# Attention values summed over two row halves, in two PSUM banks, in layers 1 to 3 of a four-layer gated cross-attention kernel

## The chip, the cores and the metric

One Trainium2 chip; the kernel runs on one of its cores. The metric is the device time of one execution in microseconds (us). A core has TensorE (PE; its weight loads are shown apart as PEld), VectorE (DVE), ScalarE (ACT), GpSimd (POOL) and SyncE (SP, which only issues DMAs here). They run side by side, each through its own instructions in order, and wait for each other by semaphores. TensorE writes its results to PSUM, which the kernel uses as eight banks of 128 rows x 512 f32 numbers; the other operands lie in SBUF.

## What is computed

Four layers, each a cross-attention and a feed-forward part, on `x` of 16 batches x 56 tokens x 256, with a context of 16 x 1500 x 64:

```python
x = x + tanh(g_xattn[l]) * xattn_l(layernorm(x), ctx)
x = x + tanh(g_ffn[l])   * ffn_l(layernorm(x))
```

In layers 1 to 3 the attention is multi-head latent attention with 16 heads. With the context `kv_rope` (rotated, 1500 x 64 for a batch), it comes down to

```python
scores = einsum('bhsr,bhlr->bhsl', q_r, k_r)       # l: 1500 keys
attn   = softmax(scores)
ctx_c  = einsum('bhsl,bld->bhsd', attn, kv_rope)   # the "values": 64 numbers a query
out    = (ctx_c through w_kc_kv) @ Wo.T
```

The kernel folds the weights so that a query is 64 numbers that meet `kv_rope` itself, for keys and for values. The feed-forward parts are a mixture of experts (layers 0, 2, 3) and an fp8-rounded matrix (layer 1). All of the attention is in f32.

## The kernel before

**Tiles and steps.** `attention_mla(l, ...)` (L698) is called for l = 1, 2, 3. The 16 batches are 8 tiles of two batches. A tile has 896 queries for each of the two batches (16 heads x 56 tokens), cut into 7 blocks of 128 (`QT`), so a layer has 56 steps `Step(t, j)`, the three layers 168. The 1500 keys are 12 chunks (`KC`) of 125 (`KP`). `kv[125, tile, chunk, batch, 64]` holds the context by keys; `kvT[128, 1500]` holds it turned, batch b in rows 64b to 64b+63.

**A step** has these parts, for both batches b = 0, 1:

- `scores` (L760): for each third z of the keys (500 of them) one matmul a batch, with 64 rows: batch 0 into bank `sp0[z]`, batch 1 into a bank of `sp1`. The two batches use different halves of TensorE's rows.
- `maxima0` (L772, L774), `maxima1` (L777) on VectorE, `exps0` (L783, three instructions) and `exps1` (L792) on ScalarE: exponentials `p` and their sums `den`.
- `invert` (L803 to L811): the sums are added on GpSimd, inverted and turned on VectorE (L805, L807), and go through DRAM by DMAs of SP's queue (L809, L811) to be repeated over 64 rows each in `rep`.
- `turned(n)`, n = 0 to 5 (L822): four 125x128 blocks of `p` are turned by TensorE into one bank, and `keep_turned(n)` copies the bank to `pT`: n = 0, 1 by VectorE (L830), the rest by ScalarE (L832).
- `values` (L840): for each chunk and batch one matmul of 125 rows, `kv` (125 x 64) as weights and `pT` (125 x 128) streaming; batch b writes rows 64b to 64b+63 of one bank, so the two batches use different halves of the columns. All 12 chunks are summed there.
- `keep` (L851): VectorE multiplies the sum by `rep` into `ctxT`, one piece a batch, two in the block j = 3 that has columns of both halves of the heads.

**Order.** It is written out by hand: `in_order` keeps the order of the program on each engine. Pass k of the loop issues the scores, maxima and first exponentials of step k, then the values of step k-2, then six times a turn of step k-1 with its copy, with `exps1` and `invert` of step k before the third. Between them, generators (`go("X")`, "Z", "R", "E") issue the parts that follow a finished tile: `project` (L863, 8 matmuls on `ctxT`), the next layer's normalisation, the router, the fp8 matrix.

**Keys of layer 1.** There `kvT` of the next tile is made on TensorE: `keys(t, z)` (L745) turns four chunks into a bank and ScalarE copies them (L748), in the passes with j = 2, 3, 4, after the scores and ahead of the first exponentials. The result is also stored (L750) and read back in layers 2 and 3.

**Banks.** Eight: `sp0` three, `sp1` three, and two that `misc()` gives in turn. Turns n = 1, 2, 3 use `sp0[0..2]`, whose exponentials are done; n = 0, 4, 5 and the values use `misc()`. The values' bank is also lent: `room(n)` gives its columns from 128 on to the generators.

## Time and profile before

| | |
|---|---|
| three runs | 2300.48, 2300.88, 2303.32 us; median 2300.88 |
| the profiled execution | 2298.12 us, its span 2296.3 us |
| TensorE's granted clock, mean over the span | 0.977; 1.00 in the stretches of the three attention layers |
| attention layers 1, 2, 3 (from the span's start) | about 335 to 820, 943 to 1365, 1619 to 2118 us |
| scores on TensorE, L760 | x2016, mean 596 ns, busy 471.7 us |
| turns on TensorE, L822 | x4032, mean 281 and 274 ns, busy 292.6 and 265.3 us |
| values on TensorE, L840 | x8064, mean 275 ns, busy 478.2 us |
| products on VectorE, L851 | x384, mean 272 ns, busy 104.3 us |
| copies of turned probabilities, ScalarE, L832 | x672, mean 595 and 619 ns |
| GpSimd in all | busy 346.3 us, 15% |

Every f32 matmul that computes shows as two instructions; a turn shows as one. The busy time of TensorE counts overlapping matmuls once, and an instruction's duration runs from its start to its modelled end, so durations of neighbours overlap: what a phase costs is read from start to start in the timeline. A timeline line merges equal instructions in a row; its columns are the start, the time to the end of the last, the engine and line, and how many. In the table of groups the last columns are the idle time of the engine just ahead of them and what ended it.

### The profile page before, as it was taken

To read this page: it belongs to the slowest core of one execution; us is meant where nothing else is said; L and a number is where in the kernel's file an instruction comes from. 1 tells how busy PE (TensorE), PEld (TensorE's weight loads), DVE (VectorE), ACT (ScalarE), POOL (GpSimd) and SP (SyncE) were. 2 spreads that over 40 slices of the span, in tenths; PEclk is the share of its full clock that TensorE was granted. 3 is DMA by queue.
4 is the path that set the end of the run, shared out by engine and by line. 5 is a ranking of instruction groups with operands and counts; after the bars stand their busy time and mean duration, and the time that the engine had idled before them with its cause. 6 is when DMAs were issued, how large, how long until landed. Compare 5 with 4: busy or idle time off the path is not lost. (4 is left out here: it accounts for less than half of the span.)

```text
span 2296.3 us, 47100 instructions
## 1 busy us (share of the span) xinstructions
PE 2198.5 (96%) x17838; PEld 1598.8 (70%) x17846; DVE 1562.3 (68%) x3627; ACT 1221.7 (53%) x2675; POOL 346.3 (15%) x678
## 2 busy tenths in 40 slices
PE   8879999999999999999999999989999999999698
PEld 5647657777777784457777777745677777777465
DVE  5658457777777878767777777624677777777332
ACT  4313357666666653366666666514666666666132
POOL 1225600000000004410000000000001111101234
PEclk9779999999999999999999999999999999999799
DMA  9545450000000002100000000154001100000465
GB/s 273 183 136 163 141 158 23 22 22 23 16 15 22 23 23 81 57 20 22 25 24 24 25 12 23 49 206 142 20 22 31 30 30 21 27 22 18 135 196 168
DMA packets 106681, 153.48 MB, mean 67 GB/s; under 512 B 18319, under 2 KB 76696, under 8 KB 105417
## 3 DMA queue, kind: packets, MB, share of 16 engines
q1 hardware_dynamic: 97299, 131.83, 18.9%
q0 software_dynamic: 7600, 17.14, 2.3%
q8 instruction: 146, 2.39, 0.4%
q10 hardware_dynamic: 1542, 1.34, 0.2%
q14 instruction: 94, 0.77, 0.1%
HBM read 111.73 MB, written 40.48 MB: 66 GB/s over the span
## 5 line engine op out<-in xcount | busy, mean ns | idle before, releaser
L783 ACT ACTIVATE p<-s_ps,nm 128x500 f32<-128x500 f32 x504 | 335.2, 674 | 402.1 <-DVE nm L774 396.3
L840 PEld LDWEIGHTS m_ps<-pT,kv 125*64 125x64 f32 x8064 | 437.0, 137 | 112.5 <-issue 108.8
L840 PE MATMUL m_ps<-pT,kv 125*64 125x128 f32 x8064 | 478.2, 275 | 3.7 <-ACT pT L832 2.5
L772 DVE TENSOR_REDUCE part<-s_ps 128x1 f32<-128x500 f32 x504 | 341.8, 678 | 203.0 <-PE s_ps L760 200.0
L760 PE MATMUL s_ps<-kvT,qT 64*128 64x500 f32 x2016 | 471.7, 596 | 3.1 <-ACT qT L330 2.6
L760 PEld LDWEIGHTS s_ps<-kvT,qT 64*128 64x128 f32 x2016 | 182.4, 186 | 179.1 <-issue 115.6
L822 PE MATMUL m_ps<-ident,p 128*125 128x128 f32 x2016 | 292.6, 281 | 2.4 <-issue 2.4
L777 DVE TENSOR_REDUCE nm<-s_ps 128x1 f32<-128x1500 f32 x168 | 287.5, 1711 | 0.0
L822 PEld LDWEIGHTS m_ps<-ident,p 128*125 128x125 f32 x2016 | 246.2, 187 | 33.6 <-issue 28.2
L822 PE MATMUL s_ps<-ident,p 128*125 128x128 f32 x2016 | 265.3, 274 | 1.5 <-ACT p L783 1.0
L792 ACT ACTIVATE p<-s_ps,nm 128x1500 f32<-128x1500 f32 x168 | 254.5, 1515 | 4.5 <-DVE nm L777 4.4
L822 PEld LDWEIGHTS s_ps<-ident,p 128*125 128x125 f32 x2016 | 241.9, 188 | 4.0 <-ACT p L783 1.6
L832 ACT COPY pT<-s_ps 125x512 f32<-125x512 f32 x336 | 180.8, 595 | 99.7 <-PE s_ps L822 87.1
L803 POOL TENSOR_TENSOR den<-den 128x1 f32<-128x1 f32 x168 | 32.5, 193 | 1325.9 <-ACT p L783 1325.7
L832 ACT COPY pT<-m_ps 125x512 f32<-125x512 f32 x336 | 185.1, 619 | 0.0
L851 DVE TENSOR_TENSOR ctxT<-m_ps,rep 64x128 f32<-64x128 f32 (+1 forms) x384 | 104.3, 272 | 65.6 <-PE m_ps L840 52.0
L1336 PE MATMUL gu_ps<-wgu,xT 128*128 128x448 f32 (+2 forms) x344 | 138.3, 528 | 4.4 <-ACT xT L1326 4.4
L830 DVE COPY pT<-m_ps 125x512 f32<-125x512 f32 x168 | 116.2, 692 | 10.5 <-PE s_ps L822 0.5
L330 ACT COPY qT<-q_ps 64x224 f32<-64x224 f32 x124 | 69.7, 562 | 98.5 <-PE q_ps L378 67.1
L1361 POOL DMA_INDIRECT results<-y,to x78 | 92.8, 1189 | 169.3 <-ACT y L1360 116.9
L830 DVE COPY pT<-s_ps 125x512 f32<-125x512 f32 x168 | 114.4, 681 | 0.0
L1341 DVE TENSOR_TENSOR act<-gu_ps,act 128x224 f32<-128x224 f32 (+2 forms) x78 | 31.3, 401 | 120.7 <-ACT act L1340 88.8
(305 smaller groups left out, 2518.4 us busy)
## 6 DMA issues: line engine op xcount, KB each, us to landing
rows<-zero SPq DMA_DIRECT2D x16, 899.5 KB
kvT<-turned_kv SPq DMA_DIRECT2D x16, 750.0 KB
rep<-through SPq DMA_DIRECT2D x336, 32.0 KB
xrow<-rows SPq DMA_DIRECT2D x78, 128.5 KB
wgu<-in_L_wgu SPq DMA_DIRECT2D x21, 448.0 KB
wgu<-in_L_wgu SPq DMA_DIRECT2D x8, 1024.0 KB
back<-results SPq DMA_DIRECT2D x16, 448.0 KB
wq<-in_L_wq SPq DMA_DIRECT2D x24, 256.0 KB
```

The costliest lines, as they stand in the source:

```text
L760: in_order(nc.tensor.matmul(o[:, 0 : 4 * KP], qT[64 * b : 64 * b + 64, t, j * QT : (j + 1) * QT], kvTs[t][64 * b : 64 * b + 64, z * 4 * KP ...
L772: in_order(nc.vector.tensor_reduce(self.part[:, z : z + 1], sp0[z][:, 0 : 4 * KP], AX.X, ALU.max))
L777: in_order(nc.vector.tensor_reduce(self.nm[1], sp1[:, :, 0 : 4 * KP], AX.XY, ALU.max, negate=True))
L783: in_order(nc.scalar.activation(self.p[0][:, 4 * z * KP : 4 * (z + 1) * KP], sp0[z][:, 0 : 4 * KP], AF.Exp, bias=self.nm[0], accum_out=sel ...
L792: in_order(nc.scalar.activation(self.p[1].rearrange("p (z c) -> p z c", z=3), sp1[:, :, 0 : 4 * KP], AF.Exp, bias=self.nm[1], accum_out=se ...
L822: in_order(nc.tensor.transpose(ps[:, c, :], self.p[b][:, k : k + KP], ident))
L830: in_order(nc.vector.tensor_copy(o, ps))
L832: in_order(nc.scalar.copy(o, ps))
L840: in_order(nc.tensor.matmul(self.pv[64 * b : 64 * b + 64, :], kv[:, self.t, c, b, :], self.pT[:, c, b, :], start=c == 0, stop=c == KC - 1))
L851: in_order(nc.vector.tensor_tensor(ctxs[self.t][64 * a : 64 * a + 64, b, lo - 448 * a : hi - 448 * a], self.pv[64 * b : 64 * b + 64, cols] ...
L1336: in_order(nc.tensor.matmul(ps[:, s, 0:n], xT[:, k, :], wgu[:, k, s * n : (s + 1) * n], start=k == 0, stop=k == 1))
L1361: i = nc.gpsimd.indirect_dma_start(flat, bass.IndirectOffsetOnAxis(ap=to[:, 0:1], axis=0), y, None, bounds_check=B * S * top - 1, oob_is_e ...
```

## The change

Five things change together:

1. **Values.** Each chunk of 125 keys is cut into rows 0 to 63 and 64 to 124. Each matmul becomes two, with 64 and 61 rows, the lower half of the keys into one `misc()` bank (`lent`), the upper into a second (`beside`). The columns stay 64 a batch.
2. **Keep.** VectorE multiplies each of the two 128x128 sums by `rep` into SBUF (`v0`, `v1`), and GpSimd adds them into `ctxT`, in the pieces of before.
3. **Score banks rotate.** The bank of third z in step i is `sp0[(i + z) % 3]`.
4. **Turns.** As the values hold both `misc()` banks, n = 0, 1, 2 and 5 use `sp0[(k + n % 5) % 3]`, and n = 3, 4 use `misc()`.
5. **Keys of layer 1.** Four parts of three chunks, in place of three of four, in the passes with j = 2 to 5, issued after the second turn into the columns from 128 on of `beside`. In layers 2 and 3 the read of the turned keys stays at j = 2.

```diff
@@ -96,7 +96,7 @@
     def misc():
         return psm.tile([128, 512], F32, tag="m", name="m_ps")
 
-    lent = [None]
+    lent, beside = [None], [None]
 
     def room(n):
 
@@ -732,31 +732,31 @@
             ctxs = {}
             nq = 8 * TP // QT
 
-            def keys(t, z):
-
-                if l > 1:
-                    if z == 0:
-                        keys_again(t)
-                    return
+            def keys(t, z, ps=None):
+
                 if z == 0:
                     kvTs[t] = kp.tile([128, L], F32, name="kvT")
-                ps = misc()
-                for c in range(4):
+                ps = (misc() if ps is None else ps[:, QT:])[:, 0 : 3 * KP]
+                for c in range(3):
                     in_order(nc.tensor.transpose(
-                        ps[:, c * KP : (c + 1) * KP], kv[:, t, 4 * z + c].rearrange("p b e -> p (b e)"), ident[0:KP, 0:KP]
+                        ps[:, c * KP : (c + 1) * KP], kv[:, t, 3 * z + c].rearrange("p b e -> p (b e)"), ident[0:KP, 0:KP]
                     ))
-                in_order(nc.scalar.copy(kvTs[t][:, z * 4 * KP : (z + 1) * 4 * KP], ps[:, 0 : 4 * KP]))
-                if z == 2:
+                in_order(nc.scalar.copy(kvTs[t][:, z * 3 * KP : (z + 1) * 3 * KP], ps))
+                if z == 3:
                     in_order(nc.sync.dma_start(turned_kv[t], kvTs[t]))
 
             class Step:
                 def __init__(self, t, j):
                     self.t, self.j = t, j
 
+                def bank(self, z):
+
+                    return sp0[(nq * self.t + self.j + z) % 3]
+
                 def scores(self, z):
 
                     t, j = self.t, self.j
-                    for b, o in enumerate((sp0[z], sp1[:, z, :])):
+                    for b, o in enumerate((self.bank(z), sp1[:, z, :])):
                         in_order(nc.tensor.matmul(
                             o[:, 0 : 4 * KP],
                             qT[64 * b : 64 * b + 64, t, j * QT : (j + 1) * QT],
@@ -769,7 +769,7 @@
                     if z == 0:
                         self.part = ap.tile([QT, 3], F32, name="part")
                         self.nm = [ap.tile([QT, 1], F32, name=f"nm{b}") for b in range(2)]
-                    in_order(nc.vector.tensor_reduce(self.part[:, z : z + 1], sp0[z][:, 0 : 4 * KP], AX.X, ALU.max))
+                    in_order(nc.vector.tensor_reduce(self.part[:, z : z + 1], self.bank(z)[:, 0 : 4 * KP], AX.X, ALU.max))
                     if z == 2:
                         in_order(nc.vector.tensor_reduce(self.nm[0], self.part, AX.X, ALU.max, negate=True))
 
@@ -782,7 +782,7 @@
                     for z in range(3):
                         in_order(nc.scalar.activation(
                             self.p[0][:, 4 * z * KP : 4 * (z + 1) * KP],
-                            sp0[z][:, 0 : 4 * KP],
+                            self.bank(z)[:, 0 : 4 * KP],
                             AF.Exp,
                             bias=self.nm[0],
                             accum_out=self.den[:, z : z + 1],
@@ -810,16 +810,17 @@
                     for b in range(2):
                         in_order(nc.sync.dma_start(self.rep[64 * b : 64 * b + 64, :], through[b : b + 1, :].to_broadcast([64, QT])))
 
-                def turned(self, n):
+                def turned(self, n, at):
+
 
                     if n == 0:
                         self.pT = ap.tile([KP, KC, 2, QT], F32, name="pT", bufs=1)
                     z, b = n // 2, n % 2
-                    ps = sp0[n - 1] if 1 <= n <= 3 else misc()
+                    ps = misc() if n in (3, 4) else sp0[(at + n % 5) % 3]
                     ps = ps[0:KP, :].rearrange("p (c q) -> p c q", c=4)
                     for c in range(4):
-                        k = (4 * z + c) * KP
-                        in_order(nc.tensor.transpose(ps[:, c, :], self.p[b][:, k : k + KP], ident))
+                        cut = slice((4 * z + c) * KP, (4 * z + c + 1) * KP)
+                        in_order(nc.tensor.transpose(ps[:, c, :], self.p[b][:, cut], ident))
                     self.turning = ps
 
                 def keep_turned(self, n):
@@ -833,26 +834,37 @@
 
                 def values(self):
 
+
+
+                    beside[0] = misc()
                     lent[0] = misc()
-                    self.pv = lent[0][:, 0:QT]
+                    self.pv = [ps[:, 0:QT] for ps in (lent[0], beside[0])]
                     for c in range(KC):
                         for b in range(2):
-                            in_order(nc.tensor.matmul(
-                                self.pv[64 * b : 64 * b + 64, :], kv[:, self.t, c, b, :], self.pT[:, c, b, :], start=c == 0, stop=c == KC - 1
-                            ))
+                            for h, keys_of in enumerate((slice(0, 64), slice(64, KP))):
+                                in_order(nc.tensor.matmul(
+                                    self.pv[h][64 * b : 64 * b + 64, :],
+                                    kv[keys_of, self.t, c, b, :],
+                                    self.pT[keys_of, c, b, :],
+                                    start=c == 0,
+                                    stop=c == KC - 1,
+                                ))
 
                 def keep(self):
 
+                    v = [ap.tile([128, QT], F32, name=f"v{h}") for h in range(2)]
+                    for h in range(2):
+                        in_order(nc.vector.tensor_tensor(v[h], self.pv[h], self.rep, ALU.mult))
                     for a in range(2):
                         lo, hi = max(self.j * QT, 448 * a), min((self.j + 1) * QT, 448 * (a + 1))
                         for b in range(2):
                             if lo < hi:
                                 cols = slice(lo - self.j * QT, hi - self.j * QT)
-                                in_order(nc.vector.tensor_tensor(
+                                in_order(nc.gpsimd.tensor_tensor(
                                     ctxs[self.t][64 * a : 64 * a + 64, b, lo - 448 * a : hi - 448 * a],
-                                    self.pv[64 * b : 64 * b + 64, cols],
-                                    self.rep[64 * b : 64 * b + 64, cols],
-                                    ALU.mult,
+                                    v[0][64 * b : 64 * b + 64, cols],
+                                    v[1][64 * b : 64 * b + 64, cols],
+                                    ALU.add,
                                 ))
 
             def project(t):
@@ -875,7 +887,7 @@
             def at(i):
                 return steps[i] if 0 <= i < n else None
 
-            for z in range(3 if l == 1 else 0):
+            for z in range(4 if l == 1 else 0):
                 keys(0, z)
             after, wanted, pending = iter(()), "X", None
 
@@ -900,8 +912,8 @@
                     for z in range(3):
                         new.scores(z)
                         new.maxima0(z)
-                    if new.t + 1 < NT and new.j in (2, 3, 4):
-                        keys(new.t + 1, new.j - 2)
+                    if l > 1 and new.t + 1 < NT and new.j == 2:
+                        keys_again(new.t + 1)
                 if k == 0:
                     late = late()
                     next(late, None)
@@ -917,13 +929,15 @@
                         new.exps1()
                         new.invert()
                     if turn:
-                        turn.turned(i)
+                        turn.turned(i, k)
                     if i == 1:
                         if pending:
                             for _ in after:
                                 pass
                             after, wanted, pending = pending, "Z", None
                         go("Z")
+                        if l == 1 and new and new.t + 1 < NT and new.j in (2, 3, 4, 5):
+                            keys(new.t + 1, new.j - 2, beside[0])
                     if turn:
                         turn.keep_turned(i)
                     if i == 1:
```

## Prediction

> **What bounds the kernel now.** I read the busy table first, then the groups of instructions, then one step of layer 1 in the timeline, then the waits of TensorE.
>
> ```profile
> PE 2198.5 (96%) x17838; PEld 1598.8 (70%) x17846; DVE 1562.3 (68%) x3627; ACT 1221.7 (53%) x2675; POOL 346.3 (15%) x678
> ...
> L840 PE MATMUL m_ps<-pT,kv 125*64 125x128 f32 x8064 | 478.2, 275 | 3.7 <-ACT pT L832 2.5
> ...
> L760 PE MATMUL s_ps<-kvT,qT 64*128 64x500 f32 x2016 | 471.7, 596 | 3.1 <-ACT qT L330 2.6
> ```
>
> TensorE is busy 96% of the span, and its two large groups sat idle for under 4 us in all. The three attention layers (335 to 820, 943 to 1365 and 1619 to 2118 us) are 1406 us, of which the table by stretches gives TensorE 1394. The timeline of TensorE shows the order; the first step here also turns keys (L745), the second does not.
>
> ```profile
> 433.07 2.79 PE L760 MATMUL s_ps<-kvT,qT 64*128 64x500 f32 x12
> 435.79 0.65 PE L745 MATMUL m_ps<-ident,kv 125*128 125x125 f32 x4
> 436.36 2.84 PE L840 MATMUL m_ps<-pT,kv 125*64 125x128 f32 x48
> 439.13 0.70 PE L822 MATMUL m_ps<-ident,p 128*125 128x128 f32 x4
> 439.67 1.47 PE L822 MATMUL s_ps<-ident,p 128*125 128x128 f32 x12
> 440.98 1.04 PE L822 MATMUL m_ps<-ident,p 128*125 128x128 f32 x8
> 441.95 2.79 PE L760 MATMUL s_ps<-kvT,qT 64*128 64x500 f32 x12
> 444.67 2.84 PE L840 MATMUL m_ps<-pT,kv 125*64 125x128 f32 x48
> 447.44 0.70 PE L822 MATMUL m_ps<-ident,p 128*125 128x128 f32 x4
> ```
>
> From start to start, scores take 2.72 us, values 2.77, the 24 turns of probabilities 2.82: 8.30 us a step, 168 steps, no wait between them. So only TensorE's own work, or a wait that reaches it, moves the time.
>
> **The values (168 steps).** An f32 matmul is two instructions, so 24 matmuls are x48. In the single records they start in pairs, 7 ns apart (the two halves of the columns), with 109 ns from pair to pair: 24 x 109 = 2.62 us, and the rest of the 2.77 is the start of the phase. 109 ns is the streaming of 128 columns: a score instruction with 500 columns and 64 rows takes 417 ns, the same 0.83 ns a column. So fewer rows don't stream faster, and two tiles of 125 x 64 already fill the array. The change makes 96 instructions of 64 (or 61) x 64 with the same 128 columns. If four run at once, as pairs do now on two column halves (L840) and on two row halves (L760), that is 24 fours x 109 = 2.62 us again: **no gain in streaming**, and two more starts of 7 ns each: 14 ns x 168 = +2.4 us. No row shows four at once. Bounds: two at a time gives 48 x 109 = 5.23 us, +2.62 x 168 = +440; below nothing I see no reason, as the array has no idle part now. I take +2.4, by the two rows that show halves running side by side.
>
> [...] The contraction here is 125 and is cut in two, so the number of matmuls doubles with it; I follow the rows above.
>
> **The change of shape.** Between two phases of one array shape the next matmul starts 2 to 3 ns after the last one's streaming ends (turns to L863, L1640); with a change of shape it is 92 to 98 ns, plus the first weight load. That holds whether rows and columns change (L760 to L840), columns alone (L376 to L378) or rows alone (L822 to L760). Scores are 64 x 128, the values become 64 x 64, the turns 128 x 128: still three changes a step, 0. If the first cost nothing, 0.145 us x 168 = 24 us would go (second rival).
>
> **The keys of layer 1 (7 tiles).** Today three of seven steps of a tile turn four chunks each ahead of the values. Such steps take 8.88 instead of 8.30: 0.58, of which 4 x 109 ns is work and 0.14 a change of shape. Afterwards four steps turn three chunks each among the turns of probabilities: 0.33 each and no change of shape. But ScalarE's queue changes too. Today its key copy goes first:
>
> ```profile
> 436.47 0.58 ACT L748 COPY kvT<-m_ps 128x500 f32<-128x500 f32 x1 [2.49 <-PE m_ps L745]
> 436.94 0.69 ACT L783 ACTIVATE p<-s_ps,nm 128x500 f32<-128x500 f32 x1
> ...
> 439.46 1.51 ACT L792 ACTIVATE p<-s_ps,nm 128x1500 f32<-128x1500 f32 x1 [0.43 <-DVE nm L777]
> ...
> 440.96 1.06 ACT L832 COPY pT<-s_ps 125x512 f32<-125x512 f32 x2
> 441.90 1.09 ACT L832 COPY pT<-m_ps 125x512 f32<-125x512 f32 x2
> ```
>
> Afterwards it stands between the exponentials L783 and L792 and waits for the keys' turns, which come after the values and eight turns. Behind it in ScalarE's queue stand L792 and the four copies L832; for them wait the next scores' second half (L792), their second chunk (first copy) and third chunk (now the last copy), and the reciprocal. For this step, without L745 ahead: values at 435.79, turns at 438.56, keys done at 439.86 (+0.16 to be seen), the copy 440.05 to 440.41, L792 to 441.91, the copies 0.48 apart, the last ending at 443.95. TensorE has its turns done and starts the next scores at 441.71; their third chunk would start at 443.48 and waits until 443.95: **about 0.5 us**. Bounds: 0 (the copy earlier by that much) to 0.9 (0.30 for L792 adds up). Per tile: 4 x (0.33 + 0.5) - 3 x 0.58 = +1.6; x 7 = **+11 us** (-3 to +22).
>
> **Banks that rotate.** In the other steps the third chunk's bank also comes free with the last copy: that ends at 442.99 above, the third chunk starts near 443.7, so 0.7 us of cover. The first turn now waits for the first exponential (done 446.4; turn at 447.44). Both hidden; each us beyond the cover would cost 168 us.
>
> **Products and sums.** VectorE: 384 products of 64x128 (272 ns) become 336 of 128x128, the same columns, so about -13 us of busy time off the path. GpSimd gains 384 additions: its rows give 193 ns for 128x1 (L803), 319 for 112x64, 723 to 833 for 112x256, so some 450 ns for 64x128, 0.9 us a step. In its queue they stand before L803 and L804, for which L805 waits; that starts at 450.13 in the second step above, and the additions let it start by about 449.5. The reciprocals travel through DMA to a product two steps later, 16 us. Hidden, except at the end of each of three layers, where L863 waits for the context (4.6 us, twice): + 0.9 x 3 = **+2.7 us** (0 to 4). SP's queue keeps its 672 small transfers; the store of turned keys is issued one step later and is not read before layer 2.
>
> **Sum.** 2.4 + 11 + 2.7 = +16 us on the profiled execution: 2298.12 us with a span of 2296.3. The median of three is 2300.88, 2.8 above it, so **2317 us**.
>
> **Rivals.**
>
> *TensorE isn't fed fast enough.* 192 instructions with their weight loads must come in 2.62 us, one in 13.6 ns. The densest stretch of that length holds 102 (25.5 ns each); L596 holds 64 at 14.6 ns, a short burst. And in layer 3 TensorE stalls for "issue" inside the values, while GpSimd scatters rows:
>
> ```profile
> 1879.01 0.27 PE L840 MATMUL m_ps<-pT,kv 125*64 125x128 f32 x1 [0.41 <-issue]
> 1879.72 0.32 PE L840 MATMUL m_ps<-pT,kv 125*64 125x128 f32 x1 [0.44 <-issue]
> ```
>
> At 14.6 ns the values take 2.80 us, +0.18 x 168 = +31, 2348 us; at 25.5 ns 4.90 us, +384, 2701 us; two at a time 2757 us.
>
> [...]
>
> *No change of shape between 64-row phases.* Faster: weight loads of the values run under the last scores, 0.145 us a step goes: 2317 - 24 = 2293 us. It decides from the point where the distance L760 to values falls under 95 ns by more than 0.1 us. Against it: a change in one dimension alone costs the same today.
>
> *The keys' copy doesn't hold the scores.* Then the 11 us become -3: 2303 us, no change that can be told.
>
> *Four tiles stream more than two,* which no row suggests: half the values' time, 2317 - 220 = 2097 us.
>
> **Chances.** Forecast (own range 2306 to 2345) 0.45; not fed 0.21 (2345 to 2757); keys not held, within 0.2%, 0.10; no change of shape 0.16 (2276 to 2296); faster streaming 0.08. So faster 0.24, within 0.2% (4.6 us, about what a measurement of this kernel can tell from no change) 0.10, slower 0.66. For the range I leave out the 0.08 below and about half of "not fed", 0.10, above 2440: 2276 to 2440.
>
> **What would show it.** The values' group: x16128, fours 7 ns apart and 109 from four to four, 2.77 to 2.80 us a phase. Steps without keys in layers 2 and 3 stay at 8.30. Layer 1's steps with keys at about 9.1, with L760 waiting for ScalarE's L792 or copies. A values phase of over 3 us with idle "issue" shows the first rival; steps near 8.16 the second. The forecast is wrong altogether if a shape of 64 x 64 streams at a rate per column other than 0.83 ns.

## The result, and the profile after

The changed kernel takes **2342.56 us** (median of 4 runs, 2341.41 to 2345.2) beside 2301.49 us for the kernel before (4 runs): ratio 1.0179, 95% interval 1.0162 to 1.0197, 41 us slower. The forecast was 2317 us: right in sign, too small by about 26 us. The profiled execution took 2345.2 us with a span of 2343.1, 46.8 us more than that of before. (It is the slowest of the four runs, and the 2298.12 us of before lie below all four of before, so the profiles are further apart than the medians.)

From the profile after, the line of busy times, then the groups of the scores, the values and the new additions (busy us, mean ns of one, idle time just before them and what ended it):

```profile
PE 2233.4 (95%) x25910; PEld 1617.4 (69%) x25910; DVE 1534.1 (65%) x3579; ACT 1223.4 (52%) x2683; POOL 507.4 (22%) x1062
...
L845 PE MATMUL m_ps<-pT,kv 64*64 64x128 f32 (+1 forms) x16128 | 492.1, 272 | 10.8 <-issue 10.6
L760 PE MATMUL s_ps<-kvT,qT 64*128 64x500 f32 x2016 | 490.0, 601 | 2.6 <-ACT qT L330 2.6
...
L863 POOL TENSOR_TENSOR ctxT<-v,v 64x128 f32<-64x128 f32 (+1 forms) x384 | 160.8, 419 | 1181.3 <-DVE v L857 1123.0
```

Three things differ from before. The values (L845, L840 before) have 10.6 us of idle time "issue" in front of them, where there were 3.7 us of idle time in all. The scores are busy for 18 us more, with the same instructions: they stretch over waits inside them. And the additions are there, 419 ns each.

A plain step (timeline of TensorE, layer 3) is what it was:

```profile
1826.35 2.79 PE L760 MATMUL s_ps<-kvT,qT 64*128 64x500 f32 x12
1829.06 2.85 PE L845 MATMUL m_ps<-pT,kv 64*64 64x128 f32 x96
1831.85 1.57 PE L823 MATMUL s_ps<-ident,p 128*125 128x128 f32 x12
...
1834.66 0.69 PE L760 MATMUL s_ps<-kvT,qT 64*128 64x500 f32 x2
```

8.31 us instead of 8.30. In the single records four matmuls start 6 to 7 ns apart and the next four 109 ns after the first; the phase takes 2.78 us from start to start (median of the 168), 2.77 before. So the time came from elsewhere. The table lays the starts of all 168 score phases of the two profiles side by side (us; the differences add up to 46.8):

| stretch | before | after | more |
|---|---|---|---|
| before the first scores | 338.0 | 339.9 | 1.9 |
| layer 1, first to last scores | 496.2 | 513.2 | 17.0 |
| layer 1's last scores to layer 2's first | 152.6 | 153.4 | 0.8 |
| layer 2, first four steps | 32.1 | 36.8 | 4.7 |
| layer 2, the rest | 455.4 | 453.9 | -1.5 |
| layer 2's last scores to layer 3's first | 144.4 | 154.0 | 9.6 |
| layer 3, first to last scores | 493.0 | 501.4 | 8.4 |
| layer 3's last scores to the end | 184.6 | 190.5 | 5.9 |

**Layer 1: the keys.** Timeline of after, a step with keys, the turns on TensorE and ScalarE's queue:

```profile
445.27 0.54 PE L741 MATMUL m_ps<-ident,kv 125*128 125x125 f32 x3 [0.17 <-DVE v L857]
...
445.85 0.48 ACT L744 COPY kvT<-m_ps 128x375 f32<-128x375 f32 x1 [1.51 <-PE m_ps L741]
446.21 1.52 ACT L792 ACTIVATE p<-s_ps,nm 128x1500 f32<-128x1500 f32 x1
...
447.49 3.43 PE L760 MATMUL s_ps<-kvT,qT 64*128 64x500 f32 x12
447.71 0.59 ACT L833 COPY pT<-s_ps 125x512 f32<-125x512 f32 x1
448.18 1.09 ACT L833 COPY pT<-m_ps 125x512 f32<-125x512 f32 x2
449.13 0.63 ACT L833 COPY pT<-s_ps 125x512 f32<-125x512 f32 x1
```

ScalarE stands idle for 1.51 us until the keys are turned; then the copy, L792 and four copies follow, the last ending at 449.76, and the next scores take 3.43 us instead of 2.79.

**Ends of layers.** Timeline of after at the end of layer 2, GpSimd and TensorE:

```profile
1511.87 3.48 PE L845 MATMUL m_ps<-pT,kv 64*64 64x128 f32 x96
1512.52 0.97 POOL L1104 DMA_INDIRECT rows<-xr,sloti  x1 [1.92 <-DVE weight L1112]
1515.94 0.45 POOL L863 TENSOR_TENSOR ctxT<-v,v 64x128 f32<-64x128 f32 x1 [2.46 <-DVE v L857]
1519.62 0.45 POOL L863 TENSOR_TENSOR ctxT<-v,v 64x128 f32<-64x128 f32 x1 [3.23 <-DMA rows<-xr,sloti]
1520.13 6.28 PE L875 MATMUL m_ps<-G,ctxT 128*112 128x256 f32 x16 [4.78 <-POOL ctxT L863]
```

The first addition runs when its product is there. The second waits until the rows of the scatter L1104 have landed, though it doesn't touch them: in the built program the wait for the scatter's rows, which before stood in front of L1019 (the next GpSimd instruction then), stands in front of this addition. The projection waits 4.78 us for it, 0.80 before, and its 16 matmuls then take 6.28 us instead of 3.79. In the profile of before, the same place (GpSimd's copy waits for the scatter, and the projection doesn't wait for the copy):

```profile
1492.96 3.79 PE L863 MATMUL m_ps<-G,ctxT 128*112 128x256 f32 x16 [0.80 <-DVE ctxT L851]
1495.98 0.18 POOL L1019 COPY xr<-small 112x1 f32<-112x1 f32 x1 [5.90 <-DMA rows<-xr,sloti]
```

The table by stretches of after (TensorE's busy time, granted clock, DMA share, GB/s) shows why:

```profile
1513.00:1518.00 5.00, 2.35 (x78) 1.00 0.99 404
1518.00:1523.00 5.00, 2.87 (x7) 0.55 0.03 9
```

In the second stretch, with the end of the wait and the first half of the projection, the granted clock is 0.55; over the projection itself it is 0.58, and 1.00 in before.

The end of layer 3 is not the same case in these two profiles. The projection of before:

```profile
2133.32 5.47 PE L863 MATMUL m_ps<-G,ctxT 128*112 128x256 f32 x16 [3.75 <-DVE ctxT L851]
```

and that of after:

```profile
2176.68 5.69 PE L875 MATMUL m_ps<-G,ctxT 128*112 128x256 f32 x16 [1.50 <-POOL ctxT L863]
```

Before already waits 3.75 us for its product there and has the slow projection, at a granted clock of 0.69. In after the last values stall and take 7.9 us instead of 2.84; the scatters have landed by then, and the wait is 1.50 us. Where the values don't stall, the second addition waits for a scatter here too: the projection waits 4.54 us in after_third and 4.55 us in keys_before below, and 0.80 us in banks_only, which has no additions.

**Layer 3: stalls inside values.** Timeline of after, the second step behind the plain one above, TensorE with the first and the last of four scatters on GpSimd:

```profile
1844.32 0.98 POOL L1104 DMA_INDIRECT rows<-xr,sloti  x1 [1.55 <-DVE is_j L1111]
...
1845.85 1.69 PE L845 MATMUL m_ps<-pT,kv 64*64 64x128 f32 x46
1847.82 0.38 PE L845 MATMUL m_ps<-pT,kv 61*64 61x128 f32 x2 [0.28 <-issue]
1848.08 0.93 POOL L1104 DMA_INDIRECT rows<-xr,sloti  x1 [0.30 <-issue]
1848.56 0.46 PE L845 MATMUL m_ps<-pT,kv 64*64 64x128 f32 x4 [0.37 <-issue]
1850.00 1.54 PE L845 MATMUL m_ps<-pT,kv 64*64 64x128 f32 x44 [0.98 <-issue]
```

Beside these scatters TensorE runs in bursts of 46, 2, 4 and 44 matmuls, with 0.28 to 0.98 us of idle time between them. In the layer's last values, which stall in the same way, about five matmuls come every 0.72 us:

```profile
2170.10 0.46 PE L845 MATMUL m_ps<-pT,kv 61*64 61x128 f32 x5 [0.27 <-issue]
2170.84 0.45 PE L845 MATMUL m_ps<-pT,kv 64*64 64x128 f32 x5 [0.28 <-issue]
```

The profile names nothing that TensorE waits for ("issue"). I read it as instructions that come too slowly; no run shows that directly. Nor is it shown that GpSimd's work is what slows them: in the stalled steps of the four profiles with split values, the last gap ends about 1 us after GpSimd's last scatter instruction, close to the end of the scatters' transfers. The steps with scatters, six in the layer, take 11.05 us on average, against 9.26 before.

**Layer 2's first steps** ran at a granted clock of 0.50 for some 7 us, and again for some 3, in this profile, which before's didn't; other profiles of the same kernel below have 33.9 and 32.5 us there. So that row is put down to chance, not to the change.

### The profile page after: what moved, and what is told of

Read it like the earlier page. It is cut to its first block, busy times and chain, and to the rows that moved or that the text cites. A ratio compares the mean times of both kernels' runs of the same rounds, so it can differ in the third digit from the quotient of the medians.

```text
span 2343.1 us, 63903 instructions
## 1 busy us (share of the span) xinstructions
PE 2233.4 (95%) x25910; PEld 1617.4 (69%) x25910; DVE 1534.1 (65%) x3579; ACT 1223.4 (52%) x2683; POOL 507.4 (22%) x1062
## 5 line engine op out<-in xcount | busy, mean ns | idle before, releaser
L845 PEld LDWEIGHTS m_ps<-pT,kv 64*64 64x64 f32 (+1 forms) x16128 | 443.5, 133 | 139.1 <-PE s_ps L760 98.2
L845 PE MATMUL m_ps<-pT,kv 64*64 64x128 f32 (+1 forms) x16128 | 492.1, 272 | 10.8 <-issue 10.6
L772 DVE TENSOR_REDUCE part<-s_ps 128x1 f32<-128x500 f32 x504 | 339.5, 678 | 184.1 <-PE s_ps L760 182.3
L863 POOL TENSOR_TENSOR ctxT<-v,v 64x128 f32<-64x128 f32 (+1 forms) x384 | 160.8, 419 | 1181.3 <-DVE v L857 1123.0
L823 PE MATMUL s_ps<-ident,p 128*125 128x128 f32 x2688 | 384.9, 280 | 3.7 <-ACT p L783 3.7
L823 PEld LDWEIGHTS s_ps<-ident,p 128*125 128x125 f32 x2688 | 329.0, 188 | 35.9 <-issue 27.9
L792 ACT ACTIVATE p<-s_ps,nm 128x1500 f32<-128x1500 f32 x168 | 254.6, 1516 | 2.3 <-DVE nm L777 2.2
L831 DVE COPY pT<-s_ps 125x512 f32<-125x512 f32 x336 | 221.9, 686 | 29.8 <-PE s_ps L823 29.2
L823 PE MATMUL m_ps<-ident,p 128*125 128x128 f32 x1344 | 175.7, 274 | 0.0
L823 PEld LDWEIGHTS m_ps<-ident,p 128*125 128x125 f32 x1344 | 160.7, 188 | 0.0
L857 DVE TENSOR_TENSOR v<-m_ps,rep 128x128 f32<-128x128 f32 x336 | 81.9, 286 | 62.0 <-PE m_ps L845 61.8
L783 ACT ACTIVATION_READ_ACCUMULATOR p<-s_ps,nm 128x1 f32 x504 | 100.6, 200 | 0.0
```

Source lines behind the costliest of these rows:

```text
L772: in_order(nc.vector.tensor_reduce(self.part[:, z : z + 1], self.bank(z)[:, 0 : 4 * KP], AX.X, ALU.max))
L783: in_order(nc.scalar.activation(self.p[0][:, 4 * z * KP : 4 * (z + 1) * KP], self.bank(z)[:, 0 : 4 * KP], AF.Exp, bias=self.nm[0], accum_o ...
L792: in_order(nc.scalar.activation(self.p[1].rearrange("p (z c) -> p z c", z=3), sp1[:, :, 0 : 4 * KP], AF.Exp, bias=self.nm[1], accum_out=se ...
L823: in_order(nc.tensor.transpose(ps[:, c, :], self.p[b][:, cut], ident))
L831: in_order(nc.vector.tensor_copy(o, ps))
L845: in_order(nc.tensor.matmul(self.pv[h][64 * b : 64 * b + 64, :], kv[keys_of, self.t, c, b, :], self.pT[keys_of, c, b, :], start=c == 0, st ...
```

## The experiments

Each set of kernels ran on one chip together with the kernel before. The kernel before takes 2301.6 us on one of these chips and 2284 to 2285 us on the others (four sets, three chips). So each run is given with its ratio to the kernel before in its own set (interval 95%); the first comparison (2301.49 us) looks like the first of these. On that chip the first scores come at 338 to 339 us in all four profiles, on the others mostly at 328 to 333.

### Set 1 (before 2285.5 us): one part at a time

**banks_only.** The kernel before with `bank(z)`, and with

```diff
-                    ps = sp0[n - 1] if 1 <= n <= 3 else misc()
+                    ps = misc() if n in (3, 4) else sp0[(at + n % 5) % 3]
```

> The kernel before with nothing but the rotated score banks and the banks of the turns as after the change; values whole, keys four chunks at a time ahead of the values. Theory: the banks are hidden, so 2301.5 us within 2 us. Rival: a bank comes free late (a copy of turned probabilities or an exponential that the scores or the turns now wait for); each 0.1 us a step costs 16.8 us, so over 2310 us, and TensorE's line of the scores or the turns shows a wait for ScalarE or VectorE in plain steps, which then take over 8.31 us.

Measured: 2283.97 us, ratio 0.9988 (0.9978 to 0.9999). Plain steps are 8.30 us; layer 1 takes 497.3 us, against 496.2 in the profile of before. The banks cost nothing, as the prediction had it; no stretch of the profile shows where 2.7 us would be gained, so I don't count them as a gain either.

**whole_values.** The kernel after, with

```diff
-                            for h, keys_of in enumerate((slice(0, 64), slice(64, KP))):
+                            in_order(nc.tensor.matmul(self.pv[64 * b : 64 * b + 64, :], kv[:, self.t, c, b, :], ...
...
-                                in_order(nc.gpsimd.tensor_tensor(...v[0]..., ...v[1]..., ALU.add))
+                                in_order(nc.vector.tensor_tensor(...self.pv..., ...self.rep..., ALU.mult))
```

> The kernel after with the values whole again (contraction of 125, 24 matmuls, one product on VectorE, no additions on GpSimd); keys in four parts of three chunks among the turns and rotated banks as after. Theory: what is left is the keys' term, which the trace of after puts at 2.4 us a tile x 7 = 17 us, where the prediction had 11: 2318 us, layer 1's steps with keys at 9.2 to 9.7 us as after. Rival 1 (the prediction's size): 2312 us. Rival 2 (the long steps of layer 1 come from the split values, not from ScalarE's queue): steps of about 8.63 us and a time of 2298 us.

Measured: 2301.41 us, ratio 1.0065 (1.0047 to 1.0083), 16 us above before and 17 above banks_only. Layer 1 takes 512.3 us, as after does with 513.2. The keys' place alone makes layer 1 longer; the split has next to no part in it.

**keys_before.** The kernel after, with the keys' three parts of four chunks back in front of the values:

```diff
+                    if l == 1 and new.t + 1 < NT and new.j in (2, 3, 4):
+                        keys(new.t + 1, new.j - 2)
...
-                            keys(new.t + 1, new.j - 2, beside[0])
```

> The kernel after with the keys turned as before the change (three parts of four chunks, ahead of the values); split values, additions on GpSimd and rotated banks as after. Theory: the keys' 17 us go and the rest stays (stalls of TensorE inside the values of layer 3 while GpSimd scatters rows, the wait of the last projection for GpSimd's addition, a lower granted clock after it): 2325 us, layer 1's key steps at 8.88 us again. Rival (the prediction's terms): 11 us go, 2332 us.

Measured: 2307.09 us, ratio 1.0092 (1.0073 to 1.011). The layer-1 steps didn't return to 8.88 us: they took 9.62. Timeline of keys_before, TensorE:

```profile
421.21 0.65 PE L741 MATMUL m_ps<-ident,kv 125*128 125x125 f32 x4
421.79 0.43 PE L845 MATMUL m_ps<-pT,kv 64*64 64x128 f32 x2
422.52 2.84 PE L845 MATMUL m_ps<-pT,kv 61*64 61x128 f32 x94 [0.30 <-ACT kvT L744]
```

The split values need both of the two spare banks (`lent` and `beside`), and the keys have just filled one: the third matmul waits for the keys' copy. So the run doesn't take the keys' term away, it puts another in its place, and the expectation of 2325 us, on the scale of the first comparison, can't be judged by it. It shows something else: with split values and no stall, the layer-3 step is 8.31 us here, where after had 11.05 on another chip.

**add_on_vector.** The kernel after, with `nc.vector` for `nc.gpsimd` in the addition.

> The kernel after with the 384 additions of the two halves on VectorE instead of GpSimd. Theory: the second addition of a layer's last step stands in GpSimd's queue behind a wait for the scatter's rows, and the idle time of TensorE there (4.8 us at the end of layer 2) is followed by a lower granted clock; on VectorE the wait goes: 4 us at layer 2's end, 1 at layer 3's, and up to 5 us of lower clock, so 2333 us (2332 to 2338). The stalls in the values of layer 3 (27 for issue, 10.6 us) stay. Rival 1 (the additions never reach the end of a layer by more than the prediction's 2.7 us): 2340 us. Rival 2 (VectorE's queue becomes late, with its maxima or copies behind the additions): over 2343 us and steps over 8.31 us.

Measured: 2328.55 us, ratio 1.0181 (1.016 to 1.0201), 43 us above before: rival 2. At both layer ends the projection waits 1.30 us instead of 3.7 to 4.8 and takes 3.79 us. But VectorE's queue is late: the steps with router work take 8.98 and 8.91 us in layer 2, against 8.72 and 8.47, and layers 1 and 3 are longer too.

### Set 2 (before 2301.6 us): repairs

**after_again.** The kernel after.

> The kernel after once more, beside the kernels of this set and of the last one, since the time of the kernel before was 2301.5 us in the first comparison and 2285.5 us in the last set. The single edits of the last set give, against the kernel before beside them, banks -2.7 us, banks with keys +15.9, banks with split values +21.6, so that all three add up to +40 us if they only add. Theory (a part of the 41 us was TensorE's stalls inside the values of layer 3 while GpSimd scatters rows, which no profile of the last set shows): the ratio is smaller here, about 1.012 to 1.016 (27 to 37 us), with steps of 8.31 us where the first profile had 11.05. Rival (the change costs the same everywhere): 1.018, 41 us.

Measured: 2342.01 us, ratio 1.0167 (1.0146 to 1.0189), as in the first comparison. Taken alone, that is the rival's number. But the kernel before takes 2301.6 us here, and the layer-3 steps with scatters take 12.01 us; after_third below, on a chip without such steps, has a smaller ratio.

**keys_after_exp.** The kernel after, with the keys' turns and copy moved:

```diff
                         new.exps1()
                         new.invert()
+                        if l == 1 and new.t + 1 < NT and new.j in (2, 3, 4, 5):
+                            keys(new.t + 1, new.j - 2, beside[0])
```

> The kernel after with the turning of three key chunks and its copy issued after the second exponential L792 instead of ahead of it. Theory: in after ScalarE stands idle for 1.1 to 1.5 us ahead of the keys' copy, with L792 and the copies of the turned probabilities behind it, and the next scores wait for the last copy; behind L792 the copy finds its keys turned. Layer 1's key steps fall from 9.2 to 9.7 us to about 8.65 and the time by 2.7 us a tile x 7 = 19 us against after. Rival (the keys' own work on TensorE, and its wait for the bank beside the values, make the step long): steps stay over 9.0 us, gain under 5 us.

Measured: 2331.33 us, ratio 1.0127 (1.0105 to 1.0148), 10.7 us less than after_again; layer 1 takes 500.5 us instead of 513.1. Timeline of keys_after_exp, the same kind of step:

```profile
440.06 1.51 ACT L792 ACTIVATE p<-s_ps,nm 128x1500 f32<-128x1500 f32 x1 [0.52 <-DVE nm L777]
441.56 0.46 ACT L744 COPY kvT<-m_ps 128x375 f32<-128x375 f32 x1
...
440.48 0.54 PE L741 MATMUL m_ps<-ident,kv 125*128 125x125 f32 x3 [0.17 <-DVE v L857]
442.08 0.70 PE L823 MATMUL m_ps<-ident,p 128*125 128x128 f32 x4 [0.18 <-ACT kvT L744]
442.62 0.60 PE L823 MATMUL s_ps<-ident,p 128*125 128x128 f32 x4
443.15 2.79 PE L760 MATMUL s_ps<-kvT,qT 64*128 64x500 f32 x12
```

The copy finds its keys turned, and the scores are back at 2.79 us. So the order in ScalarE's queue was the cause of that wait. The gain is smaller than the 19 us expected, as the steps take 8.84, 9.47, 8.85 and 8.53 us: in the longest TensorE is idle 0.17 us before the keys' turns, which wait for their bank, and 0.18 us before other turns, which wait for the keys' copy.

**last_sum_on_vector.** The kernel after, with

```diff
+                    last = self.t == NT - 1 and self.j == nq - 1
-                                in_order(nc.gpsimd.tensor_tensor(
+                                in_order((nc.vector if last else nc.gpsimd).tensor_tensor(
```

> The kernel after with the additions on VectorE only for the last step of each layer. Theory: with every addition on VectorE, TensorE's wait ahead of the last projection fell from 3.7 to 4.8 us to 1.3 us and the projection from 5.5 to 6.3 us to 3.8, as no lower clock followed; but VectorE's queue then made all steps longer. With only the last ones there the first is kept and the second goes: 5 us at the ends of layers 2 and 3 each, 10 us less than after, steps as in after. Rival (the lower clock comes at these ends whatever waits): at most 5 us less.

Measured: 2334.87 us, ratio 1.015 (1.0129 to 1.017), 7.1 us less than after_again. The two intervals overlap; the profiles show where the gain is: layer 2's last scores to layer 3's first take 145.9 us instead of 153.2. Timeline of last_sum_on_vector, end of layer 2:

```profile
1510.46 3.49 PE L845 MATMUL m_ps<-pT,kv 64*64 64x128 f32 x96
1515.23 3.79 PE L876 MATMUL m_ps<-G,ctxT 128*112 128x256 f32 x16 [1.28 <-DVE ctxT L864]
```

The long wait and the slow projection are gone together. At the end of layer 3 the stalls in the last values (7.76 us instead of 3.3) hide most of the second gain on this chip.

**whole_keys_after_exp.** whole_values with the keys of keys_after_exp.

> The kernel after with whole values (as in the run whole_values) and the keys' turns and copy after the second exponential. Theory: the key steps cost 0.33 us of TensorE's work each and nothing else, 4 x 0.33 = 1.3 us a tile, where the kernel before has 3 x 0.58 = 1.7; so 3 us less than the kernel before, and 2 to 3 us more by the banks: ratio 0.997 to 0.999. Rival (the copy after L792 makes the last copy of turned probabilities too late for the third chunk of the scores): key steps over 8.9 us, ratio over 1.003.

Measured: 2310.74 us, ratio 1.0031 (1.0019 to 1.0042): the rival's number, and its steps of over 8.9 us (up to 9.47). Layer 1 takes 502.9 us, 5.6 more than banks_only: even behind L792 the keys among the turns cost more than in front of the values, and the theory of 0.33 us a step was wrong. One wait is in the profile, and it is not the one that the rival named: turns (L823) for the keys' copy L744, 7 times, 3.7 us.

### Set 3 (before 2283.6 us): the scatters

**scatter_later.** The kernel after, with a new slot after the second maximum (after the products in a layer's last step):

```diff
             in_order(nc.vector.tensor_reduce(slot, prod, AX.X, ALU.add))
+            yield "S"
             in_order(nc.vector.tensor_copy(sloti, slot))
...
                     new.maxima1()
+                    go("S")
```

> The kernel after with one order changed: the cast that the scatters of the next feed-forward's rows wait for stands behind the second maximum of the next step on VectorE (behind the products in a layer's last step), so that GpSimd writes the four scatters while TensorE turns probabilities and makes scores, which take few instructions, and not during the values. Theory (TensorE is short of instructions while GpSimd scatters: 5 matmuls each 0.72 us): where the kernel before takes about 2301 us, the steps of 11 to 12 us in layer 3 fall to 8.3 and the last values of the layer from 7.6 us to about 3, 20 to 26 us less than after, 2316 to 2322 us, ratio 1.006 to 1.009. Where the kernel before takes about 2285 us there are no such stalls, and the time is that of after. Rival (the scatters' data or another transfer starves TensorE, not the moment of GpSimd's work): the stalls move with the scatters into the turns and scores, and the time stays within 5 us of after.

Measured: 2328.68 us, ratio 1.0186 (1.017 to 1.0203). This chip has no stalls, so the run can't tell the theories apart, and the edit made a wait of its own. Timeline of scatter_later, in GpSimd's and VectorE's queues at the following step (15.8 us; the six of the layer take 14.7 to 18.1 instead of 11.86):

```profile
1837.64 0.93 POOL L1108 DMA_INDIRECT rows<-xr,sloti  x1 [0.30 <-issue]
...
1840.43 0.45 POOL L863 TENSOR_TENSOR ctxT<-v,v 64x128 f32<-64x128 f32 x1 [1.36 <-DMA rows<-xr,sloti]
1840.96 0.19 POOL L803 TENSOR_TENSOR den<-den 128x1 f32<-128x1 f32 x1
...
1841.47 0.17 DVE L805 RECIPROCAL wide<-den 128x2 f32<-128x2 f32 x1 [5.65 <-POOL den L804]
1841.80 1.81 DVE L772 TENSOR_REDUCE part<-s_ps 128x1 f32<-128x500 f32 x3
```

The denominators' sums wait behind scatters and additions, the reciprocal L805 waits for the sums, and behind L805 in VectorE's queue the maxima of the next scores wait. I had looked only at the 16 us that the reciprocal has until its product. At the ends of layers 2 and 3, though, the moved scatters have landed in time: the projection waits 1.62 us with the additions still on GpSimd, and its 16 matmuls take 3.82 us. So the scatter, and not the addition itself, made the long wait there.

**banks_scatter_later.** banks_only with the same slot.

> The kernel before with the rotated banks alone (values whole, keys as before) and the scatters' cast moved as in scatter_later. Theory: the banks give 2.7 us (ratio 0.9988), and where the kernel before takes about 2301 us its own stalls in layer 3 go too (0.95 us in each of six steps and about 4.6 us ahead of the last projection), so 2288 to 2293 us, ratio 0.994 to 0.997; where it takes 2285 us, ratio 0.9985. Rival (moving the scatters delays the denominators' sums behind them on GpSimd until a product waits, or the start of the feed-forward after layer 3): ratio 1.000 or more.

Measured: 2288.95 us, ratio 1.0026 (1.0014 to 1.0037): the rival. The six steps behind the scatters take 12.6 to 12.7 us instead of 11.85.

**three_repairs.** The kernel after with the edits of keys_after_exp, last_sum_on_vector and scatter_later.

> The kernel after with the keys' turns and copy behind the second exponential, the last additions of a layer on VectorE, and the scatters' cast moved: the split values stay. Theory: the three repairs take back 11 us, 7 us and (where the kernel before takes about 2301 us) 20 to 26 us, which they do not share, so 2298 to 2305 us there, ratio 0.998 to 1.002, and 1.001 to 1.005 where the kernel before takes about 2285 us: the split of the values itself costs almost nothing, and gains nothing. Rival (something else in the split costs): ratio over 1.006 in both.

Measured: 2312.21 us, ratio 1.0128 (1.0109 to 1.0147). Outside the expectation, by the third repair: six steps of layer 3 take 14.7 to 18.4 us instead of 11.86, together 26 us more. (The expectation of two_repairs below has seven such steps at 3.35 us each; the profile has six, at 4.3 us on average.)

**half_values.** The kernel after, with `for h, keys_of in enumerate((slice(0, 64),))`: one half, which the second product takes once more. It leaves out 61 of every 125 keys.

> The kernel after with the values of the first 64 rows of each chunk alone: 48 instructions instead of 96 (it leaves out the other 61 rows of every chunk, so its sums are not the whole ones). It asks whether half the rows stream faster. Theory: streaming goes by columns, whatever the rows, so two tiles of 64 x 64 at once take the time of two of 125 x 64 and of four of 64 x 64: a phase of 2.77 us, pairs 109 ns apart, and plain steps of 8.30 us. Rival (a tile of 64 rows streams in half the time, and the four of after only looked like 109 ns because instructions came no faster): pairs 55 ns apart, a phase of 1.4 us, steps of 7.0 us and 220 us less.

Measured, timeline of half_values, TensorE:

```profile
1106.32 2.79 PE L760 MATMUL s_ps<-kvT,qT 64*128 64x500 f32 x12
1109.04 2.84 PE L845 MATMUL m_ps<-pT,kv 64*64 64x128 f32 x48
1111.81 1.58 PE L823 MATMUL s_ps<-ident,p 128*125 128x128 f32 x12
```

From start to start 2.77 us, steps 8.30, pairs 109 ns apart, with half the rows. A matmul of 64 rows took what one of 125 does; the split doubles the matmuls and runs two in the time of one. (Its 2395.96 us can't be compared: the experts' first product has 460 matmul instructions instead of 344, as the rows are routed by these sums; layer 2's last scores to layer 3's first are 188 us instead of 144, and the end 240 instead of 185.)

### Sets 4 and 5 (before 2284.7 and 2284.1 us): what is left

**after_third.** The kernel after.

> The kernel after once more, beside the two kernels of this set. Theory: where the kernel before takes about 2301 us, as in the two sets with it so far, ratio 1.017 with steps of 11 to 12 us in layer 3; where it takes about 2285 us no step of layer 3 is longer than 8.31 us but for router and projection, and from the segments of the profiles there (layer 1 +16 us, ends of the layers +8, the rest of layers 2 and 3 -4) the ratio is 1.008 to 1.011. Rival (the stalls have nothing to do with the difference between the sets): 1.017 in both.

Measured: 2315.05 us, ratio 1.0134 (1.0115 to 1.0153). Layer 3 takes 485.0 us, against 501.4 and 507.1 on the slower chip. Timeline of after_third, a step with scatters (the first and the last of the four shown):

```profile
1834.83 0.98 POOL L1104 DMA_INDIRECT rows<-xr,sloti  x1 [1.54 <-DVE is_j L1111]
...
1836.38 2.85 PE L845 MATMUL m_ps<-pT,kv 64*64 64x128 f32 x96
1838.59 0.93 POOL L1104 DMA_INDIRECT rows<-xr,sloti  x1 [0.30 <-issue]
1839.16 1.58 PE L823 MATMUL s_ps<-ident,p 128*125 128x128 f32 x12
```

The same instructions at the same places, and no stall. The ratio is smaller than on the slower chip but above the 1.008 to 1.011 expected: in this profile the stretch ahead of the first scores, which the change doesn't touch, is 339.5 us long instead of 328 to 333, and I can't say why.

**two_repairs** and **two_repairs_again.** The kernel after with the edits of keys_after_exp and last_sum_on_vector.

> The kernel after with the keys' turns and copy behind the second exponential and the last additions of a layer on VectorE; scatters where they were. Theory: the two gains, 11 and 7 us, add, and nothing waits for a delayed scatter as in three_repairs (there 3.35 us in each of seven steps): where the kernel before takes 2301 us, 2324 us, ratio 1.009 to 1.011, the rest being stalls in layer 3; where it takes 2285 us, ratio 1.002 to 1.004. Rival (the split values themselves cost more than their starts): ratio over 1.007 where the kernel before takes 2285 us, with plain steps over 8.31 us.

> two_repairs once more, for the case that the kernel before takes about 2301 us in this set: theory 2324 us, ratio 1.009 to 1.011, with steps of 11 to 12 us in layer 3 where the kernel mixed has about 9.2, so that the stall goes with the number of TensorE's instructions. If the kernel before takes about 2285 us, 1.0012 again and no such step in either. Rival (the stall does not go with the number of instructions): the same long steps in both kernels.

Measured: 2287.49 us, ratio 1.0012 (1.0000 to 1.0024), and 2287.78 us, ratio 1.0022 (1.0010 to 1.0034). Both fell on a chip without stalls, so the second settles no more than the first. Against after_third, on the same chip, the repairs take back 27.6 us; in the profiles 12.6 in layer 1, 6.4 between layers 2 and 3, 4.3 at the end, and 7.6 ahead of the first scores, which neither edit touches. All that is left is 3 to 4 us, and layer 1, at 500.5 us against 497.3 in banks_only, has as much: with keys and layer ends repaired, the split itself costs nothing that these runs can tell.

**whole_where_scattered.** two_repairs, with whole values for `l == 3 and self.j == nq - 1`.

> The kernel two_repairs with whole values (48 instructions and one product) in one step of seven, and in layer 3 alone: the step during whose values GpSimd scatters four times. Theory (with a given stretch of slow supply, the stall grows with the number of instructions that the values need): where two_repairs has steps of 11 to 12 us there, they fall to the 9.2 us of the kernels with whole values, 2.8 x 6 = 17 us and 2 to 4 us in the layer's last step less than two_repairs. Where the kernel before takes 2285 us nothing changes, within 3 us. Rival (the stall is a wait for something that the number of instructions does not change): within 5 us of two_repairs in both.

Measured: 2289.28 us, ratio 1.0011 (0.9998 to 1.0023), as two_repairs: nothing to shorten where nothing stalls. Inconclusive.

**mixed.** Banks rotated; layer 1 as in banks_only; in layers 2 and 3 split values but for `self.j == nq - 1`.

> Rotated banks; layer 1 with whole values and keys as before the change; layers 2 and 3 with split values and additions on GpSimd, but whole values in each tile's last step, so that no addition stands ahead of a projection. Theory: layer 1 as in banks_only (497 us from first to last scores), layers 2 and 3 as in two_repairs (1.4 and 2.7 us shorter than with whole values, since the steps with router work are 0.2 us shorter), ends of the layers as before: 3 to 7 us less than the kernel before where that takes 2285 us, ratio 0.997 to 0.9985. Where it takes 2301 us the steps with scatters keep whole values and about 9.2 us, so the same ratio. Rival (the shorter router steps come from the additions' place in the tile's last step, or the change between whole and split values costs bank waits): ratio 1.000 or more.

Measured: 2284.87 us, ratio 1.0002 (0.9992 to 1.0012). Layers 2 and 3 keep the gain of the router steps (8.72 instead of 8.92, 8.47 instead of 8.53 and 8.74), 1.5 and 2.8 us against banks_only, but the whole is no faster than before. No kernel tried is clearly faster than the kernel before.

## Why the prediction was wrong, step by step

The forecast was +16 us; the medians give +41, the profiles +46.8. In the profiles the three ends of the layers have 16.3 us more (0.8, 9.6 and 5.9) where the sum had 2.7, the keys of layer 1 have 17.0 where it had 11, and the steps with scatters in layer 3 have about 11 where it had nothing.

**The values: right.** No gain in streaming and some 14 ns more a phase; measured fours 109 ns apart and 10 ns. half_values shows the reason that the prediction gave: with half the rows, pairs still came 109 ns apart, so the time did not go by the rows. two_repairs closes the account from the other side: with keys and layer ends repaired, 0.12 to 0.22% is left.

**The changes of shape: right.** From the end of the scores' streaming to the first value is still 92 ns in the trace of after, so the second rival (2293 us) didn't happen.

**Keys of layer 1: the right mechanism, undersized.** +17.0 us in the profile where the step said +11. The term was "about 0.5 us" for the wait of the third chunk; it measures up to 0.64 (3.43 instead of 2.79), some 4 us more over 28 steps. The keys' turns also wait 0.17 us for the products to leave their bank (six times, 1.0 us), which I hadn't listed. Moving the copy behind L792 gave 10.7 us back, 12.6 in layer 1 of the profiles, so ScalarE's order is shown as the cause of most of it.

**Products and sums: the step that failed.** "Hidden, except at the end of each of three layers, where L863 waits for the context: +0.9 x 3 = +2.7 us (0 to 4)" counted two additions' duration and took their queue as free. In every profile with these additions and the scatters in place, the second addition at the end of layer 2 waits for a scatter to land, the projection waits 3.7 to 5.0 us (0.80 before), and its matmuls then take 1.4 to 2.5 us longer (in after 6.28 us at a granted clock of 0.58, in before 3.79 us at 1.00). The same happens at the end of layer 3 where the values don't stall (4.5 us in after_third and keys_before); in the first comparison they stall there, and take 5 us more than before. The "4.6 us, twice" that the prediction quotes were 0.80 us at layer 2 and 3.75 us at layer 3. last_sum_on_vector took 7.1 us off on the slower chip, and with the scatters moved (scatter_later) the long waits were gone too. I had written myself that every queue a step is moved past counts, and named L803 and L804; the scatters in the same queue I left out. Their rows' wait was in the profile of before, at L1019, where nobody waited for it.

**"TensorE isn't fed fast enough": the rival happened in part.** It was priced as an all-or-nothing case. In fact plain steps have no gap (192 instructions with weight loads in 2.78 us), and the stalls come only beside the scatters, almost all of them in layer 3, in the first comparison and on the chip of set 2. "168 steps, no wait between them" was therefore read from plain steps alone: before, six steps of layer 3 take 9.0 to 9.8 us. The two lines that I showed for it (0.41 and 0.44 us) were such stalls, and with twice the instructions they should have been doubled in the forecast: before loses about 0.95 us in each of six steps (in four of them in the turns behind the values), the split kernel 2.7 to 3.7. On the chip where nothing stalls (after_third) the change costs 30 us, on the slower one 40 to 41: about 10 us of the miss. That the stall grows with the number of instructions rests on six profiles that have stalls (whole values 9.19 and 9.26 us, split ones 11.05 to 12.01); the experiment made for it met no stall. **What stays open** is what TensorE lacks in them, why one chip has them, and whether another moment for the scatters would cure them.

**Banks: right** (0.9988). (The two groups' idle time in the prediction's first lines is 3.7 and 3.1 us, 6.8 in all, not under 4.) The rest of the 41 us is not assigned one by one: half clock in layer 2's first steps, which some profiles have and others not, and a stretch ahead of the attention that takes 328 to 340 us in these profiles without any edit in it.

## What to carry to other kernels

Here pairs of matmuls with 128 columns came 109 ns apart with 125 rows (before) and with 64 (half_values), so the cut along the contracted rows bought nothing; count what such a cut adds in banks, sums and instructions instead. When work goes to an idle engine, read what else its queue waits for at the places where somebody waits for the new work: here a DMA wait that held up nobody before came to stand in front of it. And put a copy into an in-order queue at the place where its input is ready, not where its producer was issued: 1.5 us of idle ScalarE were 0.6 us of TensorE here.

## What the hardware showed that I hadn't expected

Waits of a few microseconds came with a lower granted clock. The 16 matmuls of L875 took 3.79 to 3.82 us after waits of 0.5 to 1.6 us, 5.2 to 6.3 us after waits of 3.7 to 7.8 us, and 5.7 to 6.4 us after waits of 1.1 to 1.5 us where the values ahead had stalled for 4 to 5 us; in the table by stretches the clock falls to 0.50 to 0.58 after such idle time. How long it then stays low differs: between layers 2 and 3 it was 10 us in banks_only and 20 us in whole_values, and that stretch took 144.3 us in the one and 148.4 in the other with the same code in it.

A long wait was not needed for a lower clock: in after the clock fell to 0.50 at 2173.9 us, at the end of layer 3, and stood there until 2180.7 us; the values just ahead had come in bursts with gaps of at most 0.96 us.

The same program had TensorE stalling for "issue" beside the scatters on one chip (and in the first comparison) and not on another: five matmuls each 0.72 us, against 96 in 2.85 us. The cause is not known.
